# A two-layer vision tower on one core: how the chosen rows of the layer-0 feed-forward are turned

## The chip, the cores and the metric

The kernel runs on one core of one Trainium2 chip, in one launch. The metric is the device time of the whole execution in microseconds (us). Before the change three runs took 1913.69, 1913.17 and 1910.04 us; the median is 1913.17 us.

## The reference, cut to what matters

32 images become 256 tokens of 256 features each. They pass a tokenizer, layer 0 (attention, then a feed-forward part) and layer 1 (attention, then an expert feed-forward part). All data are 32-bit floats. The change touches one product of the layer-0 feed-forward, the one with `w1`:

```
# x: 32 images x 256 tokens x 256 features, after a layer norm
weights = einsum('bsd,do->bso', x, wr) + br          # one weight per token
idx     = top_k(weights, 128)[:, :127]               # 127 tokens of each image
sel     = x[idx]                                     # rows chosen
h       = gelu(sel @ w1 + b1)                        # 256 -> 1024
y       = (h @ w2 + b2) * weights[idx]               # 1024 -> 256
out     = zeros.at[idx].set(y) + x
```

For `sel @ w1` the kernel puts features on partitions (they are summed over) and tokens on the free axis, but the chosen rows lie in memory with tokens on partitions. So they must be turned.

## The kernel before, in words

An image is kept as a tile of 128 partitions (tokens) by 2 by 256. The kernel runs five stages one after the other: A, the tokenizer; B, layer-0 attention with the ranking of tokens; C, the layer-0 feed-forward; D, layer-1 attention; E, the layer-1 feed-forward. The order of the instructions on each engine is that of the program text, in A to D: a hand-written order, with no planner. Each engine and each DMA queue takes its instructions in that order.

**Stage B** goes by pairs of images, in steps `t` of 0 to 17. A step holds work of several pairs: the first products of pair `t`, the attention of pair `t-1`, the output of pair `t-2`, and the ranking of earlier pairs. Pair `t+1` is prepared in the same step. `blocks_b` (L262) turns its tokens with VectorE block transposes: each square of 32 partitions by 32 elements is transposed in place. The result goes to DRAM and comes back with four transfers each way (`turned_b`), so that features lie on partitions. The ranking gives each token its place, and an indirect DMA writes the tokens to a DRAM tensor `ranked` in the order of rank. The first 128 rows of `ranked` are what stage C needs.

**Stage C** goes by quads of four images, eight quads, in steps `t` of 0 to 31. The table `ORDER_C` (L877) is the written order: a row `(step, function, half)` means that the function runs for quad `u` in step `4u + step`, and within a step the rows run in the order of the table. For a quad:

- `first_ranks` (step -8; for quads 0 and 1 in stage B) loads the 128 first rows of four images to a tile `cs` (two buffers) with four transfers on the SP queue.
- `turn_c` (step -1; for quad 0 in the last step of stage B) does eight TensorE transposes of 128 by 128 to two PSUM banks, and copies them to the tile `xsel`, one with ScalarE and one with VectorE.
- `hidden_c` (steps 0 and 1) multiplies by `w1`: 16 products of 128 by 128 with 128 by 512 (the four images' 128 tokens side by side), each followed by a ScalarE gelu.
- `made` (steps 2 and 3, two images each) multiplies by `w2`. VectorE adds the bias into a tile `cy`, and the SP queue writes `cy` to DRAM as `results`.
- `fetch` (steps 4 and 5) gathers `results` back by rank with indirect DMAs of GpSimd, and `update` (steps 5 and 6) adds them to the token tile `h` on VectorE and takes the statistics for the next layer norm.

So in steady state TensorE does, for a quad: transposes, the second `made` of the quad before, two halves of `hidden_c`, the first `made`. There is one `xsel` tile. From step 8 on, a few small products that prepare weights for the later stages (`prepare`) are put between the steps. At the border of B and C the SP queue loads the weights of the later stages, some twenty transfers, and steps 0 and 1 still rank the last images.

Of the kernel before, what the change touches and what calls it, by code (L numbers as in the profile page):

```python
# [33 lines left out]
F32 = mybir.dt.float32  # L34
# [6 lines left out]
P = 128  # L41
B, N, D = 32, 256, 256
NC = N // P
# [37 lines left out]
def vit_tower(tc, a, out):  # L81

    nc = tc.nc
# [7 lines left out]
    ident = cpool.tile([P, P], F32, name="ident")  # L91
# [5 lines left out]
    def bank():  # L97
        return ppool.tile([P, 512], F32, name="bank", tag="bank")
# [16 lines left out]
    def mm(o, lhsT, rhs, first=True, last=True):  # L115
        nc.tensor.matmul(o, lhsT, rhs, start=first, stop=last)  # L116
# [63 lines left out]
    def transposed(xT, xs, copy):  # L180
# [3 lines left out]
        for k in range(2):  # L184
# [4 lines left out]
                    nc.tensor.transpose(p[:, o : o + P], x[:, c, k * P : (k + 1) * P], ident)  # L189
            copy(k, xT[:, k, :], p[:, 0:w])  # L190

    def copy_split(k, o, i):
        if k == 0:
            nc.scalar.copy(o, i)
        else:
            nc.vector.tensor_copy(o, i)
# [6 lines left out]
    px = passing_x.enter_context(tc.tile_pool(name="c_x", bufs=1, reuse_waits="tile"))  # L203
    pdram = passing_x.enter_context(tc.tile_pool(name="c_d", bufs=1, space=bass.MemoryType.DRAM))
# [8 lines left out]
    p0 = region_c0.enter_context(tc.tile_pool(name="c_0", bufs=1, reuse_waits="tile"))  # L213
# [4 lines left out]
    quads = [Quad() for _ in range(B // 4)]  # L218
# [3 lines left out]
        for j in range(4):  # L222
            nc.sync.dma_start(s.x[:, j, :], ranked[b0 + j][0:P, :])

    def turn_c(b0, s, _):
        s.xsel = p0.tile([P, 2, 4 * P], F32, name="xsel")
        for k in range(2):
            p = bank()
            for j in range(4):
                nc.tensor.transpose(p[:, j * P : (j + 1) * P], s.x[:, j, k * P : (k + 1) * P], ident)  # L230
            copy_split(k, s.xsel[:, k, :], p)

    wpool = region.enter_context(tc.tile_pool(name="w_c", bufs=1))
    region_b = ExitStack()
# [26 lines left out]

    def blocks_b(b0, s):  # L262
        s.d = pdram.tile([32, 16 * NC, 4, 32], F32, name="b_turned", bufs=2)
        y = px.tile([P, 8, 2 * NC, 32], F32, name="b_blocks", bufs=1)
        for j, x in enumerate(s.xs):
            nc.vector.transpose(
                y[:, :, j * NC : (j + 1) * NC, :].rearrange("p f c t -> p c f t"),
                x.rearrange("p c (f t) -> p c f t", t=32),
            )
        for i in range(4):  # L270
            nc.sync.dma_start(s.d[:, :, i, :], y[32 * i : 32 * i + 32].rearrange("p f c t -> p (f c) t"))

    def turned_b(b0, s, pool, name):
        s.xT = pool.tile([P, 2, 2 * N], F32, name=name)
        d = s.d.rearrange("q (k f c) i p -> f q k (c i p)", k=2, f=4)
        for f in range(4):
            nc.sync.dma_start(s.xT[32 * f : 32 * f + 32], d[f])
# [12 lines left out]
    with (  # L290
# [7 lines left out]
        for k, n in enumerate(PARTS):  # L298
            f = sum(PARTS[:k])
            x, w = pw.tile([P, n, N], F32, name=f"patch0_{k}"), pw.tile([P, n, D], F32, name=f"tokW{k}")  # L300
# [4 lines left out]
        p = bank()  # L305
# [62 lines left out]
        for b in range(B):  # L368
# [6 lines left out]
            if b == 4:  # L375
                wuv, row_b, wo, row_c, before, w1 = layer_0_weights()
# [45 lines left out]
    with (  # L422
# [96 lines left out]
        for t in range(B // 2 + 2):  # L519
            new, old, older, next_one = pair(t) if t else None, pair(t - 1), pair(t - 2), pair(t + 1)  # L520
            next_one = next_one if t else None
            if t == 1:
                turn_b(*new, p2, "bxT")
            if t >= 4:
                turned = turn_weights(2 * (t - 4))
            if old:
                scores_b(*old)
            if new:
                base_b(*new, p2.tile([P, 2 * N], F32, name="base"))
            if t >= 4:  # L530
                ranks(2 * (t - 4), turned)
                if t in (5, 7):
                    first_ranks(2 * t - 10, quads[t // 2 - 2], 0)
            if new:
                queries_b(*new, p2.tile([P, 2 * N], F32, name="bq"), p2.tile([P, 2 * N], F32, name="bk"))
            if old:
                gates_b(*old)
            if t == 1:
                factors_b(*powers)
            if next_one:  # L540
                norm_b(*next_one)
                blocks_b(*next_one)
            if old and t >= 3:
                norms_c(2 * (t - 3))
            if old:
                values_b(*old)
            if next_one:
                bias_b(*next_one)
            if old and t >= 3:
                residuals_c(2 * (t - 3))  # L550
            if next_one:
                turned_b(*next_one, p2, "bxT")
            if older:
                gated_b(*older)
                if t == B // 2 + 1:
                    turn_c(0, quads[0], 0)
                    norms_c(2 * (t - 3))
                    residuals_c(2 * (t - 3))
                output_b(*older)
# [77 lines left out]
    for i in range(2):  # L637
        s, t = slice(i * HD, (i + 1) * HD), slice((1 - i) * HD, (2 - i) * HD)
# [192 lines left out]
    with region_c:  # L831
        st_d = new_stats("d")

        def hidden_c(b0, s, half):
            if half == 0:
                s.hT = p2.tile([P, 8, 4 * P], F32, name="hT")
            for m in range(4 * half, 4 * half + 4):
                p = bank()
                for k in range(2):
                    mm(p, w1[:, k, m * P : (m + 1) * P], s.xsel[:, k, :], k == 0, k == 1)  # L840
                nc.scalar.activation(s.hT[:, m, :], p, AF.Gelu_apprx_tanh, bias=col("b1", m))

        def made(b0, s, half):
            for j in range(2 * half, 2 * half + 2):
                p = bank()
                for m in range(8):
                    mm(p[:, 0:D], s.hT[:, m, j * P : (j + 1) * P], w2[:, m, :], m == 0, m == 7)
                y = p2.tile([P, D], F32, name="cy", bufs=4)
                nc.vector.tensor_tensor(y, p[:, 0:D], row_c("b2"), ALU.add)
                nc.sync.dma_start(results[b0 + j][:], y)  # L850

        def fetch(b0, s, half):
            s.y = s.y if half else []
            for b in range(b0 + 2 * half, b0 + 2 * half + 2):
                y = px.tile([P, NC, D], F32, name="cx", bufs=8)
                for c in range(NC):
                    k = b * NC + c
                    nc.gpsimd.indirect_dma_start(
                        y[:, c, :], None, results[b][:], bass.IndirectOffsetOnAxis(rank_of[:, k : k + 1], 0)
                    )  # L860
                s.y.append(y)

        def update(b0, s, half):
            for j in range(2 * half, 2 * half + 2):
                b = b0 + j
                st, rs, i = at(st_d, b)
                for c in range(NC):
                    k = b * NC + c
                    nc.vector.scalar_tensor_tensor(  # L869
                        H[b][:, c, :], s.y[j][:, c, :], w_kept[:, k : k + 1], H[b][:, c, :], ALU.mult, ALU.add  # L870
                    )
                    stats(st, i, c, H[b][:, c, :])
            pow_rstd_of(st_d, b0 + 2 * half, 2)

        ORDER_C = ((0, hidden_c, 0), (1, hidden_c, 1), (2, made, 0), (-1, turn_c, 0), (-8, first_ranks, 0),  # L877
                   (3, made, 1), (4, fetch, 0), (5, fetch, 1), (5, update, 0), (6, update, 1))

        def step_c(t):  # L880
            for at_step, do, j in ORDER_C:
                u, r = divmod(t - at_step, 4)
                if r == 0 and 0 <= u < B // 4 and (u > 1 or do is not first_ranks):
                    do(4 * u, quads[u], j)

        END_C = 4 * (B // 4 - 1) + 4
        pairs = [Pair() for _ in range(B // 2)]
        preparing = prepare()
        for t in range(END_C):
            if t == 0:  # L890
                norms_c(B - 2)
                residuals_c(B - 2)
            if t == END_C - 2:
                for u in range(2):
                    norm_d(2 * u, pairs[u], px, "cx", 8)
            step_c(t)
            if t < 2:
                ranks(B - 4 + 2 * t, turn_weights(B - 4 + 2 * t))
            if t >= 8:
                next(preparing, None)  # L900
        passing.close()
# [152 lines left out]
    with (  # L1054
# [452 lines left out]
        p = bank()  # L1507
# [278 lines left out]
def _layout(i):  # L1786


    def blocks(w, p=P):
        k, m = w.shape[0] // p, w.shape[1]  # L1790
        return w.reshape(k, p, m).transpose(1, 0, 2)

    def column(v, p=P):
        return v.reshape(-1, p).T

# [29 lines left out]
    def pairs(w):  # L1825
# [12 lines left out]
        "rows_e": np.concatenate([rows_e[n] for n in ROWS_E]),  # L1838
        "wuv": blocks(i["L0_attn_W_uv"]),
        "wo": blocks(i["L0_attn_W_o"]),  # L1840
        "w1": blocks(i["L0_ffn_w1"]),
        "w2": blocks(i["L0_ffn_w2"]),
        "before": before,
        "wk1": blocks(i["L1_attn_Wk1"]),
# [44 lines left out]
```

## Time and profile before

| What | Value |
|---|---|
| Runs | 1910.04, 1913.17, 1913.69 us, median 1913.17 |
| Profiled execution, its own time | 1911.49 us |
| Its span | 1909.7 us |
| Mean granted TensorE clock | 0.987 |
| TensorE busy | 1864.9 us (98% of the span) |
| VectorE busy | 1313.2 us (69%) |
| ScalarE busy | 805.8 us (42%) |
| GpSimd busy | 757.6 us (40%) |
| Stage C on TensorE | about 681 to 918 us of the span |
| DMA packets | 132226, 109.17 MB |

The profile is of one execution. Its tables name engines as PE (TensorE products), PEld (TensorE weight loads), DVE (VectorE), ACT (ScalarE), POOL (GpSimd) and SPq (the DMA queue of SyncE). L116 is the line of the helper `mm` that issues all products, L230 the line of the transposes in `turn_c`, L189 that of other transposes. A float product appears in the records as two matmuls. Matmuls are pipelined, so the duration of one is longer than the distance to the next; the chain of waits (the work that ended last, followed back from the end) gives the time that they take together. The time of a DMA runs from its issue to its landing.

### The profile page before, as it was taken

The numbers are of one execution on the slowest core, as the hardware profiler recorded it, in microseconds if no ns is written. First come the engines' busy times: TensorE is split into PE (matmuls) and PEld (weight loads), VectorE is DVE, ScalarE is ACT, GpSimd is POOL, SyncE is SP. The second block draws the span as 40 slices with busy tenths as digits, with TensorE's granted clock in tenths as the row PEclk, the third lists the DMA queues.
The fourth block names the chain that finished last, engine by engine and source line by source line (L and its number), as shares of the span: only waits on it lengthen the run. The fifth ranks groups of instructions, "written<-read, shape, count | busy, mean of one in ns | idle before, by whom it ended". The sixth has DMA issues, their size and how long they took to land.

```text
span 1909.7 us, 36912 instructions
## 1 busy us (share of the span) xinstructions
PE 1864.9 (98%) x14740; PEld 1323.7 (69%) x14740; DVE 1313.2 (69%) x3271; ACT 805.8 (42%) x1632; POOL 757.6 (40%) x792
## 2 busy tenths in 40 slices
PE   9999999999999999999989999999999999999993
PEld 8887566666676776766645555567888878787872
DVE  2335478787878563534465555544999999999998
ACT  0001222121212112122334444447787888888772
POOL 1224233333434253424343433324454545555553
PEclk9999999999999999999999999999999999999995
DMA  9550121212121042212000000001222222222211
GB/s 312 151 156 18 35 61 46 71 42 58 47 54 44 34 136 63 82 54 61 15 20 1 1 1 0 1 18 24 58 52 62 58 57 63 52 63 53 64 44 57
DMA packets 132226, 109.17 MB, mean 57 GB/s; under 512 B 67792, under 2 KB 110288, under 8 KB 131664
## 3 DMA queue, kind: packets, MB, share of 16 engines
q1 hardware_dynamic: 125328, 89.17, 17.4%
q0 software_dynamic: 6144, 16.79, 2.8%
q8 instruction: 118, 1.93, 0.4%
q10 hardware_dynamic: 576, 0.79, 0.1%
q14 instruction: 60, 0.49, 0.1%
HBM read 53.75 MB, written 28.31 MB: 43 GB/s over the span
## 4 chain that ended last, share of the span: by engine, by line
PE 94%; DVE 4%; issue 1%; ACT 0%; DMA 0%; SPq 0%; POOL 0%; DVEq 0%; ACTq 0%
PE bank L116 91%; PE bank L792 2%; PE bank L189 1%; PE bank L230 0%; PE bank L500 0%; DVE six L124 0%; DVE fout L1387 0%; DVE fout L1401 0%; DVE eo L1265 0%; DMA b_turned<-b_blocks 0%; DVE ranges L1288 0%; DVE six L987 0%; DVE fout L1390 0%; DMA bxT<-b_turned 0%; DVE h L869 0%
## 5 line engine op out<-in xcount | busy, mean ns | idle before, releaser
L1184 POOL TENSOR_SCALAR_AFFINE_SELECT et<-et 128x512 f32<-128x512 f32 (+1 forms) x192 | 166.2, 878 | 201.6 <-ACT et L1175 199.7
L1175 ACT ACTIVATE et<-bank 128x512 f32<-128x512 f32 x384 | 207.7, 630 | 30.7 <-PE bank L116 30.2
L116 PE MATMUL bank<-ev,et 128*64 128x68 f32 (+1 forms) x6144 | 198.9, 225 | 0.0
L116 PEld LDWEIGHTS bank<-ev,et 128*64 128x64 f32 x6144 | 191.5, 137 | 5.7 <-issue 4.7
L116 PE MATMUL bank<-g,sx 64*128 64x512 f32 (+1 forms) x512 | 177.6, 486 | 0.0
L116 PE MATMUL bank<-g,sw 64*128 64x512 f32 (+1 forms) x512 | 177.2, 486 | 0.0
L116 PE MATMUL bank<-tokW,patch 128*128 128x256 f32 x768 | 167.6, 381 | 0.0
L116 PEld LDWEIGHTS bank<-tokW,patch 128*128 128x128 f32 x768 | 146.6, 191 | 21.4 <-DMA tokW<-in_tokW_dram 0.7
L116 PE MATMUL bank<-bxT,w_wuv 128*128 128x512 f32 x300 | 133.0, 598 | 2.5 <-DMA bxT<-b_turned 2.5
L1204 ACT COPY eo<-bank 128x280 f32<-128x280 f32 x256 | 96.0, 396 | 68.3 <-PE bank L116 61.6
L116 PEld LDWEIGHTS bank<-g,sx 64*128 64x128 f32 x512 | 93.1, 187 | 31.6 <-issue 22.7
L116 PE MATMUL bank<-wvo,dm 128*128 128x512 f32 x256 | 114.3, 599 | 0.0
L116 PE MATMUL bank<-attn,bv 128*128 128x256 f32 x512 | 113.1, 379 | 0.0
L116 PE MATMUL bank<-w_wo,gT 128*128 128x256 f32 x512 | 113.1, 379 | 0.0
L116 PE MATMUL bank<-w_w,hT 128*128 128x256 f32 x512 | 113.1, 379 | 0.0
L116 PE MATMUL bank<-xsel,w_w 128*128 128x512 f32 x256 | 111.4, 593 | 0.0
L116 PEld LDWEIGHTS bank<-attn,bv 128*128 128x128 f32 x512 | 97.2, 190 | 19.6 <-issue 7.2
L124 DVE BATCH_NORM_STATS2 six<-h 128x6 f32<-128x256 f32 x256 | 105.5, 412 | 4.4
L116 PEld LDWEIGHTS bank<-w_w,hT 128*128 128x128 f32 x512 | 96.6, 190 | 15.3 <-issue 2.9
L116 PEld LDWEIGHTS bank<-g,sw 64*128 64x128 f32 x512 | 93.1, 187 | 20.1 <-issue 9.9
L116 PEld LDWEIGHTS bank<-w_wo,gT 128*128 128x128 f32 x512 | 97.2, 190 | 13.2
L116 PE MATMUL bank<-w_wuv,bxT 128*128 128x512 f32 x240 | 105.4, 592 | 0.0
(276 smaller groups left out, 3712.6 us busy)
## 6 DMA issues: line engine op xcount, KB each, us to landing
patch<-in_patches_dram SPq DMA_DIRECT2D x31, 768.0 KB, 4.6
sw<-sx SPq DMA_DIRECT2D x64, 128.0 KB, 2.3
out_dram<-fout SPq DMA_DIRECT2D x32, 256.0 KB, 2.4
both<-fxT SPq DMA_DIRECT2D x62, 128.0 KB, 2.4
both<-hx SPq DMA_DIRECT2D x62, 128.0 KB, 2.3
b_turned<-b_blocks SPq DMA_DIRECT2D x56, 128.0 KB, 3.3
bxT<-b_turned SPq DMA_DIRECT2D x56, 128.0 KB, 3.1
cs<-ranked SPq DMA_DIRECT2D x32, 128.0 KB, 3.5
```

The source lines that it names most:

```text
L116: nc.tensor.matmul(o, lhsT, rhs, start=first, stop=last)
L124: nc.vector.bn_stats(six, x)
L189: nc.tensor.transpose(p[:, o : o + P], x[:, c, k * P : (k + 1) * P], ident)
L792: nc.tensor.transpose(p[:, o : o + P], x[:, c, k * P : (k + 1) * P], ident)
L1175: nc.scalar.activation(t2[:, i, :], p, AF.Exp)
L1184: nc.gpsimd.affine_select(out=own, in_=own, pattern=[[0, 2 * n_e], [1, P]], compare_op=ALU.is_ge, fill=0.0, base=0, channel_multiplier=-1,)
L1204: nc.scalar.copy(im.o[:, g * OC : (g + 1) * OC], p[:, 0:OC])
```

## The change

`turn_c` is replaced by two functions. `blocks_c` transposes a quad's 128 by 1024 tile by squares of 32 on VectorE, in one instruction, into a tile `blocks` (the buffer that stage B uses for the same purpose), and writes it to a DRAM tensor with one transfer on the SP queue, 4 KB from each partition. `moved_c` reads it back into `xsel` with one transfer on the SP queue, in rows of 1 KB, four per partition. After this, feature `128k + 32f + q` lies on partition `4q + f`. The rows of `w1` are put into the same order when the inputs are laid out (`turned`). A quad's tokens now lie in `xsel` in pieces of 32 elements, and the products with `w1` read them as a pattern of 4 by 4 by 32 in place of 512 elements in a row. For quad 0 both functions run in step 15 of stage B (`t == B // 2 - 1`), for the others in steps -3 and -2 of the quad.

```diff
+    def blocks_turned(y, xs, d):
+        y5 = y.rearrange("p (f s t) -> p s f t", f=4, t=32)
+        n = 8 // len(xs)
+        for j, x in enumerate(xs):
+            nc.vector.transpose(
+                y5[:, j * n : (j + 1) * n], x.rearrange("p c (k f t) -> p (c k) f t", k=2, f=4)
+            )
+        nc.sync.dma_start(d.rearrange("i q x -> (i q) x"), y)
+
+    def moved(xT, d):
+        nc.sync.dma_start(xT, d.rearrange("i q (f x) -> (q f) i x", f=4))
+        return xT.rearrange("p i (s k t) -> p k s i t", k=2, t=32)
...
-    def turn_c(b0, s, _):
-        s.xsel = p0.tile([P, 2, 4 * P], F32, name="xsel")
-        for k in range(2):
-            p = bank()
-            for j in range(4):
-                nc.tensor.transpose(p[:, j * P : (j + 1) * P], s.x[:, j, k * P : (k + 1) * P], ident)
-            copy_split(k, s.xsel[:, k, :], p)
+    def blocks_c(b0, s, _):
+        s.d = pdram.tile([4, 32, 4 * N], F32, name="c_turned", bufs=2)
+        blocks_turned(px.tile([P, 4 * N], F32, name="blocks", bufs=1), [s.x], s.d)
+
+    def moved_c(b0, s, _):
+        s.f = moved(p0.tile([P, 4, 2 * P], F32, name="xsel"), s.d)
...
-        y = px.tile([P, 8, 2 * NC, 32], F32, name="b_blocks", bufs=1)
+        y = px.tile([P, 4 * N], F32, name="blocks", bufs=1)
+        y = y.rearrange("p (f c t) -> p f c t", f=8, t=32)
...
+            if t == B // 2 - 1:
+                blocks_c(0, quads[0], 0)
+                moved_c(0, quads[0], 0)
             if older:
                 gated_b(*older)
                 if t == B // 2 + 1:
-                    turn_c(0, quads[0], 0)
                     norms_c(2 * (t - 3))
...
-                    mm(p, w1[:, k, m * P : (m + 1) * P], s.xsel[:, k, :], k == 0, k == 1)
+                    mm(p, w1[:, k, m * P : (m + 1) * P], s.f[:, k], k == 0, k == 1)
...
-        ORDER_C = ((0, hidden_c, 0), (1, hidden_c, 1), (2, made, 0), (-1, turn_c, 0), (-8, first_ranks, 0),
+        ORDER_C = ((0, hidden_c, 0), (1, hidden_c, 1), (2, made, 0), (-3, blocks_c, 0), (-2, moved_c, 0), (-8, first_ranks, 0),
                    (3, made, 1), (4, fetch, 0), (5, fetch, 1), (5, update, 0), (6, update, 1))
...
+    def turned(w):
+        w = blocks(w)
+        return w.reshape(4, 32, *w.shape[1:]).swapaxes(0, 1).reshape(w.shape)
...
-        "w1": blocks(i["L0_ffn_w1"]),
+        "w1": turned(i["L0_ffn_w1"]),
```

## The prediction

> **What bounds the kernel.** I read the page first (engine shares), then the chain of waits over stage C, then the tiles concerned, then the timeline around one turn.
>
> The chain, in its lines of start, length and piece, shows TensorE alone through a quad:
>
> ```profile
> PE 1864.9 (98%) x14740; PEld 1323.7 (69%) x14740; DVE 1313.2 (69%) x3271; ACT 805.8 (42%) x1632; POOL 757.6 (40%) x792
> ...
> 826.17 0.87 PE bank L230 x8
> 827.04 27.55 PE bank L116 x96
> 854.59 0.87 PE bank L230 x8
> 855.46 27.55 PE bank L116 x96
> 883.01 0.87 PE bank L230 x8
> ```
>
> 827.04 + 27.55 = 854.59: the pieces touch. A quad of stage C takes 28.42 us, of which 27.55 are products and 0.87 the eight transposes, and nothing is waited for. So what leaves TensorE here leaves the span, if no wait takes its place. From 827.04 to 854.59 the others have room: VectorE is busy 9.69 us, ScalarE 5.72, GpSimd 10.18 of 27.55, the DMA engines 26%.
>
> The groups of the turn, with min/median/max ns of one:
>
> ```profile
> L230 PE MATMUL bank<-ident,cs x64: 272/273/307, 673.9 to 883.6; 128*128 128x128 f32 x64
> L194 ACT COPY xsel<-bank x9: 585/585/586, 166.7 to 883.5; 128x512 f32<-128x512 f32 x9
> L196 DVE COPY xsel<-bank x9: 669/680/693, 168.4 to 887.6; 128x512 f32<-128x512 f32 x9
> L266 DVE STREAM_TRANSPOSE b_blocks<-cx x28: 661/685/707, 185.1 to 584.6; 128x512 f32<-128x512 f32 x28
> ```
>
> A transpose lasts 273 ns but eight pass in 0.87 us, 109 ns each; the 0.87 is what can be won. The block transpose that the change uses is already there in stage B, at half the size.
>
> The timeline where the new transfer must fit (start, length, engine, idle before in brackets):
>
> ```profile
> 851.17 0.42 DVE L849 TENSOR_TENSOR cy<-bank,rows_c 128x256 f32<-128x256 f32 x1 [9.54 <-PE bank L116]
> 851.62 3.77 SPq L850 DMA_DIRECT2D results<-cy  x2
> ...
> 854.42 1.04 PE L230 MATMUL bank<-ident,cs 128*128 128x128 f32 x8
> 854.62 0.42 DVE L849 TENSOR_TENSOR cy<-bank,rows_c 128x256 f32<-128x256 f32 x1 [3.03 <-PE bank L116]
> ```
>
> The second `results` transfer ends its issue at 851.62 + 3.77 = 855.39, 0.97 us after TensorE finished the first `made` (854.42, where the transposes start). `moved_c` is next on SP.
>
> The transfers that resemble the new ones (size, median us to landing):
>
> ```profile
> patch<-in_patches_dram SPq DMA_DIRECT2D x31, 768.0 KB, 4.6
> b_turned<-b_blocks SPq DMA_DIRECT2D x56, 128.0 KB, 3.3
> bxT<-b_turned SPq DMA_DIRECT2D x56, 128.0 KB, 3.1
> cs<-ranked SPq DMA_DIRECT2D x32, 128.0 KB, 3.5
> results<-cy SPq DMA_DIRECT2D x32, 128.0 KB, 1.7
> ```
>
> **What the Trainium skill says.** "TensorE: Matmul & The Clock Gate", Part 4: PE-mode transpose, says that TensorE is the only path that turns 128 by 128 in one go, that the result is in PSUM and must be copied out, and that one took about 275 ns in a kernel. The trace agrees (273 ns, copies of 585 and 680 ns), but its chain shows 109 ns each when eight follow one another. "VectorE: DVE Perf Modes", The three transpose paths, says that VectorE turns only squares of 32; hence the trip through DRAM. "DMA: Bandwidth & Descriptors", Anatomy of one DMA — SWDGE (gpsimd) path, gives a fixed part of about 2.0 us plus bytes over 436 GB/s. For 512 KB that would be 2.0 + 1.2 = 3.2 us, an estimate. The trace is near it for another kind of queue: 1.7 us at 128 KB where the formula gives 2.3, 4.6 at 768 KB where it gives 3.8. "Advanced Engine Details and Errata", SBUF Cachelines, says that reads keep full speed while following accesses stay in a line of 16 bytes; pieces of 32 floats (128 bytes) do. No run here shows such short pieces on TensorE.
>
> **The change, part by part.**
>
> *Removed from TensorE:* the chain has eight such pieces, seven of 0.87 and one of 0.93 (at 765.90): 7.02 us. For quads 1 to 7 there is no cover, each counts in full. For quad 0 (674.03) the next product needs `gT`, whose four VectorE multiplications run from 673.12 to 675.60. The first is done by about 673.8 and the second by 674.4. Without transposes the product starts at 674.03 and touches the second half about 0.86 us later (four records of 0.215), so I expect no stall; if it waits for both at its start, 0.4 us of the gain is lost. Removed: 6.6 to 7.0.
>
> *Removed from ScalarE and VectorE:* a copy of 585 and one of 680 ns per quad. ScalarE idled 6.7 us before its copy. Worth nothing.
>
> *Added to VectorE:* one block transpose of 1024 elements per quad. Twice the 685 ns row is 1.37 us; if part of the 685 is fixed, less, 1.1 at the lowest. I take 1.3, so VectorE gains 0.6 us per quad. In its order the transpose stands after the second `made`'s two bias additions and before `update`. There VectorE waits 1.20 us for a gather before the update at 835.61, so the transpose fills a hole. Were it not covered, 1.3 us would meet the 9.54 us idle before the next `cy` at 851.17. Queued behind it are that update and GpSimd's small power; nobody on the path. In step 15 of stage B it stands at about 623.9 and pushes a `gT` multiplication from 624.93 by some 0.3 us; VectorE idles 1.03 us before each of the next three. In step 1 of stage C it is tighter: VectorE is busy from 685.19 to 701.50 but for 0.88 us before 696.46. The transpose takes that hole and delays the rest by 0.4, so the bias addition at 701.08 comes later; the next one (703.37) had 1.88 us of idle. Nothing on the path.
>
> *Added to SP:* the write, then the read. The write (512 KB) is issued after the four `cs` loads, which end at about 836.7, and has until about 855.4: 19 us for some 4 us. In step 1 it comes behind the weights (the queue is at 697.3) and lands by about 702, before `moved_c` at about 703.5. At step 15 the queue is empty until 652.9. Only quad 1 is close, by 1.5 us. Two more issues of 0.4 to 0.7 us (patch 0.37, bxT 0.59) delay `results`, whose next waits are for VectorE anyway. While SP waits for the write's landing or for `xsel`, the second `made`'s `results` stand behind it; `fetch` needs them only a step later.
>
> *The read is the critical new step.* It waits for the `results` issue (0.97 us after the first `made`); `xsel` has been free since `hidden_c` ended, 6.9 us before. Then 512 KB in rows of 1 KB. From the rows above: 1.7 us at 128 KB and 4.6 at 768 KB, both in rows of 1 KB, give 1.7 + 384/640 × 2.9 = 3.4 us. The lower bound is 1.7, the size of 128 KB; the upper bound 5.5, as four `cs` loads issued within 1.96 us land (last issue at about 1.5, plus up to 3.9 in that stretch). I take 4.0: landing at 0.97 + 4.0 = 5.0 us. `hidden_c` needs it when the second `made` ends, 27.55 / 4 = 6.89 us. Hidden, with 1.9 us to spare, by the second `made`; at the upper bound still 0.4. Without this cover it would cost its excess seven times (quad 0's is moved some 45 us ahead).
>
> *The products with w1* read pieces of 32. The only other broken moving operand is in layer 1, two pieces of 128 floats:
>
> ```profile
> L116 PE MATMUL bank<-g,sx 64*128 64x256 f32 x256 | 66.0, 377 | 0.0
> L116 PE MATMUL bank<-sx,A 64*128 64x256 f32 x512 | 60.9, 376 | 0.0
> ```
>
> 377 ns against 376 for one in a row: no price. I take none for pieces of 32; the bound above is the second rival.
>
> *Sum:* −7.0 us, 0 for the rest. On the profiled execution: 1911.49 − 7.0 = 1904.5 us (span 1909.7 to 1902.7). The median stands 1.7 us above the profiled time, so 1913.17 − 7.0 = 1906.2; I predict 1906.3, since quad 0 may lose a little.
>
> **Rivals.**
>
> *The read lands late* (10%). For it: it is issued on the last possible occasion, behind a transfer that waits for VectorE, and the `cs` loads of the same bytes reach 4.7 us each. Against it: `fetch` starts only at 860.83, so the DMA engines carry little else at that time. The gain is eaten when it lands 7.9 us after the first `made` (7 × 1.0); a little late, at 7.5, leaves 7.0 − 7 × 0.6 = 2.8: 1910.4 us.
>
> *Short pieces slow the products* (5%), the one on the slow side. The w1 products take 256 records × 0.43 = 110 us of the chain. At 6.4% (430 to 457 ns start to start) the gain is gone. At 12% the balance is +13.2 − 7.0 = +6.2: 1919.4 us. For it: no run shows pieces of 128 bytes. Against it: the two-piece form and the skill's page.
>
> *The gain is partly refilled* (9%): small waits at quad 0, at the crowded VectorE of step 1 and at the start of stage D, 3 us of 7: 1909.2 us. Against it: VectorE and GpSimd in those places wait for TensorE, and so move with it.
>
> **How the numbers follow.** The main case has 76% at 1906.3, own range 1903 to 1908.5 (the runs before spread 3.7 us). About 0.2% (3.8 us) is what a measurement of this kernel tells from no change. Faster: the main case, 75%, and part of the third and first rivals, 5%. Same: most of the first and half of the third, 13%. Slower: the second and a read far too late, 7%. Range 1902.5 to 1911: it takes in the third rival and the mild part of the first; the second and the rest lie above.
>
> **What would show it.** Right: no pieces of L230; quads of 27.55 in the chain from 711 on, touching; a block transpose of 1.1 to 1.4 us on VectorE; the read landing 3.4 to 5.5 us after issue; w1 products still at 592 ns. Wrong: a DMA into `xsel` as releaser of TensorE in the chain, with 0.5 us or more; w1 products above 592 ns; `results` issued visibly later, with VectorE or GpSimd named in the chain of stage C.

## The result, and the profile after

The changed kernel takes 1906.38 us (median of ten runs, 1903.11 to 1906.82), the kernel before 1912.66 (ten runs, 1910.04 to 1914.14). The ratio is 0.9965, with a 95% interval of 0.9955 to 0.9974. The profiled execution took 1904.97 us with a span of 1903.3; the prediction had 1906.3 for the median and 1904.5 for the profiled execution.

The chain of waits through stage C, after a line of the page with the engines' busy times. L514 is the turn of the ranking weights (L500 before), L786 a turn in the preparation of weights, L189 the first turn of layer 1:

```profile
PE 1856.5 (98%) x14676; PEld 1318.8 (69%) x14676; DVE 1311.6 (69%) x3271; ACT 801.1 (42%) x1624; POOL 757.5 (40%) x792
...
670.18 0.44 PE bank L514 x4
670.61 20.77 PE bank L116 x80
691.38 0.44 PE bank L514 x4
691.82 6.87 PE bank L116 x16
698.69 0.44 PE bank L514 x4
699.12 96.58 PE bank L116 x397
795.70 0.44 PE bank L786 x4
796.14 118.82 PE bank L116 x424
914.96 0.45 PE bank L189 x4
```

The pieces touch (670.61 + 20.77 = 691.38, 796.14 + 118.82 = 914.96), and the 0.87 pieces of the turn are gone. TensorE waits for nothing in the stage. From the last pair's first weight turn to the first turn of layer 1 it is 914.96 − 670.18 = 244.78 us. The same two marks in the kernel before:

```profile
666.69 0.44 PE bank L500 x4
...
918.34 0.45 PE bank L189 x4
```

Before it was 918.34 − 666.69 = 251.65 us. The stage gave 6.87 us.

The instructions and transfers that the change touches, as the answers by tile have them (min/median/max ns of one), with the times from issue to landing of the read (L203) in the last line:

```profile
L197 DVE STREAM_TRANSPOSE blocks<-cs x8: 1233/1236/1244, 627.3 to 860.2; 128x1024 f32<-128x1024 f32 x8
L116 PE MATMUL bank<-xsel,w_w x256: 592/592/677, 684.4 to 900.6; 128*128 128x512 f32 x128
...
L203 SPq DMA_DIRECT2D xsel<-c_turned x8: 371/376/1355, 631.2 to 881.5; - x8
...
DMA to landing us min/median/max: 3.7/3.9/4.9
```

And the timeline of one turn, where the read must fit:

```profile
825.45 0.42 DVE L865 TENSOR_TENSOR cy<-bank,rows_c 128x256 f32<-128x256 f32 x1 [3.03 <-PE bank L116]
...
826.33 0.37 SPq L203 DMA_DIRECT2D xsel<-c_turned  x1
...
832.16 4.03 PE L116 MATMUL bank<-xsel,w_w 128*128 128x512 f32 x9
...
832.70 1.23 DVE L197 STREAM_TRANSPOSE blocks<-cs 128x1024 f32<-128x1024 f32 x1
```

The bias addition at 825.45 starts 0.2 us after TensorE ends the first `made`. The read is issued at 826.33, lands 3.9 us later at 830.2, and is needed at 832.16: 1.9 us to spare. The slowest of the seven, issued at 853.87, took 4.9 us and landed at 858.8 for products at 859.70: 0.9 us to spare.

The spans differ by 6.4 us, not by 6.87, since two places outside the stage differ between these two executions. Stage A ends some 3.5 us later in the changed kernel's profile: its first patches land later, and the products behind them start at a lower granted clock (0.84 from 9 to 20 us). A stretch of layer 1 is 3.0 us longer in the profile of before. The second profiles below show that neither belongs to a kernel.

### The profile page after: what moved, and what is told of

Same layout as the page of the kernel before. It is cut to its first block, busy times and chain, and to the rows that moved or that the text cites. A ratio compares the mean times of both kernels' runs of the same rounds, so it can differ in the third digit from the quotient of the medians.

```text
span 1903.3 us, 36813 instructions
## 1 busy us (share of the span) xinstructions
PE 1856.5 (98%) x14676; PEld 1318.8 (69%) x14676; DVE 1311.6 (69%) x3271; ACT 801.1 (42%) x1624; POOL 757.5 (40%) x792
## 4 chain that ended last, share of the span: by engine, by line
PE 94%; DVE 4%; DMA 1%; issue 1%; ACT 0%; SPq 0%; POOL 0%; DVEq 0%; ACTq 0%
PE bank L116 91%; PE bank L808 2%; PE bank L189 1%; DMA patch<-in_patches_dram 0%; PE bank L514 0%; DVE six L124 0%; DVE fout L1403 0%; DVE fout L1417 0%; DVE eo L1281 0%; DMA b_turned<-blocks 0%; DVE ranges L1304 0%; DMA bxT<-b_turned 0%; DVE six L1003 0%; DVE fout L1406 0%; DVE h L885 0%
## 5 line engine op out<-in xcount | busy, mean ns | idle before, releaser
L857 ACT ACTIVATE hT<-bank,cols 128x512 f32<-128x512 f32 x64 | 44.0, 687 | 186.7 <-PE bank L116 186.7
L116 PEld LDWEIGHTS bank<-w_w,hT 128*128 128x128 f32 x512 | 97.1, 190 | 15.4 <-issue 2.9
```

## The experiments

Times are against the changed kernel's 1906.4. Ratios are against the kernel before, run beside each experiment on the same chip; the medians of the kernel before lay within 1 us of 1912.7 there.

**The turns put back as dead work.**

```diff
+    def dead_turns(b0, s, _):
+        for k in range(2):
+            p = bank()
+            for j in range(4):
+                nc.tensor.transpose(p[:, j * P : (j + 1) * P], s.x[:, j, k * P : (k + 1) * P], ident)
...
-        ORDER_C = (..., (2, made, 0), (-3, blocks_c, 0), ...
+        ORDER_C = (..., (2, made, 0), (-1, dead_turns, 0), (-3, blocks_c, 0), ...
```

> The changed kernel, with the eight TensorE transposes of each quad put back where they were, into two PSUM banks that nobody reads; the new transfers stay, the copies stay out. Theory (the gain is TensorE's time of the turns, and the read is hidden): 8 x 0.87 us come back, 1906.4 + 7.0 = 1913.4, no difference from the kernel before, and the pieces of 0.87 stand again in the chain. Rival (part of the gain came from the copies that left ScalarE and VectorE, or from another place): 1908 to 1911, below the kernel before by what the copies were worth.

Measured: 1913.37 us, ratio 1.0001 (0.9992 to 1.0009). For quad 0 the same function runs in the last step of stage B. The chain of this kernel:

```profile
667.96 0.44 PE bank L520 x4
...
827.44 0.87 PE bank L250 x8
828.31 27.55 PE bank L116 x96
855.86 0.87 PE bank L250 x8
...
919.61 0.45 PE bank L189 x4
```

The pieces of 0.87 are back, the stage takes 919.61 − 667.96 = 251.65 us as before, and nothing of the gain is left. So all of it was TensorE's time; the copies that left ScalarE and VectorE, and the transfers that came, are worth nothing here.

**The read issued without cover.**

```diff
-        ORDER_C = (..., (-2, moved_c, 0), (-8, first_ranks, 0), (3, made, 1), (4, fetch, 0), ...
+        ORDER_C = (..., (-8, first_ranks, 0), (3, made, 1), (-1, moved_c, 0), (4, fetch, 0), ...
```

> The changed kernel, with the read issued after the second made of the quad before instead of after its first, so that no product lies between it and the products with w1. Theory (issue 1.0 us after TensorE, landing 3.9 us later, and the second made's 6.9 us are the whole cover): TensorE waits 4.9 us in each of seven quads, less where the small weight products of three or four quads lie between: about 30 us, 1936 us, with the DMA into xsel as releaser of TensorE. A clock that falls in such waits could add some us. Rival (the read is covered by something else as well, as by products queued ahead): under 10 us.

Measured: 1967.78 us, 61.4 us slower than the changed kernel, twice what was expected. Two of the seven waits in the timeline:

```profile
714.86 16.54 PE L116 MATMUL bank<-xsel,w_w 128*128 128x512 f32 x32 [4.97 <-DMA xsel<-c_turned]
...
869.92 15.83 PE L116 MATMUL bank<-xsel,w_w 128*128 128x512 f32 x32 [7.80 <-DMA xsel<-c_turned]
```

The first quad waits 4.97 us, as worked out. The later ones wait 5.5 to 7.8, because the read now takes 4.5 to 6.9 us in the chain instead of 3.9. Gathers and the loads of `cs` are issued around it there (from 861.44 and at 863.50, the read at 863.03); that they slow it was not tried. All seven waits sum to 44.6 us. Small weight products stand before only two of them and covered 1.2 and 1.9 us there. The second surprise is in the length of each line (its second number): the products after a wait take 15.4 to 16.5 us for 32 records where the changed kernel's take 13.9 to 14.0. The seven together are some 13.6 us longer, and the mean granted clock over these records is 0.84 to 0.91. 44.6 + 13.6 = 58.2 of the 59.8 us by which the stage is longer (971.68 − 667.12 = 304.56). The cover is real, and a wait of TensorE costs some 30% more than its length here (13.6 beside 44.6).

**The read issued early.**

```diff
-        ORDER_C = (..., (2, made, 0), (-3, blocks_c, 0), (-2, moved_c, 0), ...
+        ORDER_C = (..., (-2, moved_c, 0), (2, made, 0), (-3, blocks_c, 0), ...
```

> The changed kernel, with the read issued before the first made's results in SP's order, 7 us earlier. Theory (hidden already): no change, 1906.4 within 2 us. Rival (the late read costs some tenths of a us per quad, hidden in the chain as products): 2 to 5 us faster, 1902 to 1904.

Measured: 1905.47 us, ratio 0.9962 (0.9948 to 0.9975) beside 0.9965 for the change. The stage takes 911.96 − 667.16 = 244.80 us. No difference: the late place of the read costs nothing.

**The read done twice.**

```diff
+        xT = p0.tile([P, 4, 2 * P], F32, name="xsel")
+        if b0:
+            moved(xT, s.d)
+        s.f = moved(xT, s.d)
```

> The changed kernel, with the read of quads 1 to 7 done twice, the second into the same tile after the first has landed. Theory (cover of 6.9 us, 1.0 used before the issue): the second lands at 1.0 + 2 x 3.9 + about 0.1 = 8.9 us after the first made, 2.0 us late in each of the quads without small weight products in between: 7 x 2.0 = 14 us at most, 10 us if three quads are covered; 1916 to 1921 us. Rival (the margin is really near zero, so that the whole second read is late): 7 x 3.9 = 27 us, 1933.

Measured: 1922.04 us, 15.6 us slower than the changed kernel and just above the range that the theory gave. Two of five waits in the timeline:

```profile
714.39 13.97 PE L116 MATMUL bank<-xsel,w_w 128*128 128x512 f32 x32 [2.13 <-DMA xsel<-c_turned]
744.16 14.00 PE L116 MATMUL bank<-xsel,w_w 128*128 128x512 f32 x32 [1.99 <-DMA xsel<-c_turned]
```

Five quads wait 2.13, 1.99, 2.17, 3.22 and 2.44 us, 11.9 in all, and two wait for nothing, as small weight products lie between. One stretch of products after a wait is 1.7 us longer (15.70). That makes 13.6 of the 15.6; the other 2 us are within the spread of the runs. Three of the waits are near the 2.0 that the sum of cover and landing gives; in the other two the reads took longer in the chain (4.97 and 4.18 us, 4.03 and 4.29). So the spare 1.9 us of the changed kernel is confirmed from the other side.

**The pieces of the moving operand.** Three kernels read the same 512 columns in another order, in pieces of one, two and four floats. The line of 16 bytes in the expectations is the one that the prediction cites from the Trainium skill.

```diff
-        return xT.rearrange("p i (s k t) -> p k s i t", k=2, t=32)
+        return xT.rearrange("p i (s k t) -> p k t s i", k=2, t=32)                 # pieces of one
+        return xT.rearrange("p i (s k a b) -> p k a (i s) b", s=4, k=2, b=2)       # of two; of four with b=4
```

> The changed kernel, with the products with w1 reading their moving operand as 32 by 4 by 4 instead of 4 by 4 by 32, so that each float comes from another place, 1 KB from the last. The 512 columns are the same in another order, so the rows of the four images of a quad are mixed in the feed-forward part: only the time is read. Theory (broken reads cost nothing at the pace of float products here, 430 ns for 512 columns): 592 ns per record and 1906 us, no change. Rival (a read pays per line of 16 bytes, and pieces of 32 floats only hid it): each of 256 records gets longer; at twice the time 256 x 0.43 = 110 us, 2016 us.

Measured: 2015.58 us, 109 us slower than the changed kernel.

> The changed kernel, with the moving operand of the products with w1 read in pieces of two floats, each 256 bytes from the last. As with pieces of one, the 512 columns come in another order, so the four images' rows are mixed in the feed-forward part; only the time is read. Theory (a second access to the same line of 16 bytes makes up for the first): 592 ns per record and 1906 us. Rival (each change of line costs, in proportion): half of the price of pieces of one, 592 + 215 = about 810 ns per record and 1961 us.

Measured: 1903.76 us, ratio 0.9954 (0.9940 to 0.9967).

> As before with pieces of four floats, a full line of 16 bytes; the images' rows are mixed in the same way. Theory: 592 ns per record and 1906 us. Rival (in proportion): 592 + 108 = about 700 ns per record and 1934 us.

Measured: 1905.34 us, ratio 0.9960 (0.9946 to 0.9973). The products with `w1` in the kernel with pieces of one:

```profile
L116 PE MATMUL bank<-xsel,w_w x256: 1019/1037/1086, 682.6 to 1008.9; 128*128 128x512 f32 x128
...
696.98 13.77 PE bank L116 x16
```

The last line is of its chain, where the changed kernel has 6.87 us for the same sixteen. With pieces of two:

```profile
L116 PE MATMUL bank<-xsel,w_w x256: 592/593/680, 682.6 to 899.7; 128*128 128x512 f32 x128
```

A record of pieces of one takes 1037 ns instead of 592. From start to start it is 13.77 / 16 = 0.86 us instead of 0.43, and 256 × 0.43 = 110 us is what the stage lost (1023.74 − 668.42 = 355.32 us instead of 244.78). Pieces of two cost next to nothing: their stage takes 914.07 − 668.41 = 245.66 us, 0.9 us more than the changed kernel's, or 3 ns per record. Pieces of four cost nothing (912.99 − 668.20 = 244.79). So the rival of the prediction that ended on the slow side exists as a mechanism, but only at single floats. (The pieces of one lie 1 KB apart and those of two 256 bytes; whether the distance plays a part was not tried.)

**The two kernels again, for second profiles.**

> The kernel before, unchanged, for a second profile. The two profiles at hand differ in two places the change doesn't touch: the first patches land 3.5 us later in the changed kernel's profile, and a stretch of layer-1 attention (1000 to 1010) runs at a granted clock of 0.67 in the profile of before alone. Theory (both are of the single execution): this profile shows other values in at least one of the two. Rival (both belong to the kernels): the clock falls again at about 1000, and the start is as fast as before.

> The changed kernel, unchanged, for a second profile. Theory: stage C from the first weight turn of the last pair to the first turn of layer 1 takes 244.8 us again (251.7 before), whatever the start and the clock do. Rival: the start of the kernel is 3.5 us later again and the clock does not fall, so that these belong to the change.

Measured: 1913.35 us (before) and 1906.33 (after). In the stretch of layer 1 the first profile of before has in its chain

```profile
1000.45 20.83 PE bank L116 x62
```

and the second

```profile
1003.77 17.84 PE bank L116 x62
```

The changed kernel's two profiles have 17.84 and 20.87 there. So each kernel shows both values: after the same wait for `dxT` the granted clock over these records is 0.85 in some executions and 1.00 in others, which makes 3.0 us. The second profile of before also waits for its first patches (6.81 us in the chain, products going on from 8.69), as both of the changed kernel do. The stage between the markers is 919.94 − 668.28 = 251.66 us and 913.42 − 668.63 = 244.79. The difference of 6.87 repeats to 0.01 us; the late start and the fall of the clock are of the single execution, as both kernels show them.

**The same turn in layer-1 attention.** Pairs 2 to 15 of stage D get block transposes, one write and one read as well.

```diff
...
+        def blocks_d(b0, s):
+            s.d = pdram.tile([4, 32, 4 * N], F32, name="d_turned", bufs=2)
+            blocks_turned(px.tile([P, 4 * N], F32, name="blocks", bufs=1), s.xs, s.d)
+
+        def moved_d(b0, s):
+            if b0 > 2:
+                s.f = moved(p2.tile([P, 4 * N], F32, name="dxT").rearrange("p (i x) -> p i x", i=4), s.d)
+            else:
+                turn(b0, s)
...
-                    mm(p, (wk1, wq1)[i][:, k, m * P : (m + 1) * P], s.xT[:, k, :], k == 0, k == 1)
+                    mm(p, ((wk1, wq1) if b0 <= 2 else (wk1t, wq1t))[i][:, k, m * P : (m + 1) * P], s.f[:, k], k == 0, k == 1)
...
-                do(1, turn)
+                do(1, moved_d)
...
-                do(0, norm_d, p8, "dx", 4)
+                do(-1, norm_d, p8, "dx", 6)
+                do(-1, blocks_d)
...
```

> The changed kernel, with the same turn in layer-1 attention for pairs 2 to 15: normalised tokens one step earlier (six buffers for four), block transposes, one write, one read, a second set of the first-layer weights in the new order of features; pairs 0 and 1 keep TensorE's transposes. Theory (same mechanism, 0.87 us per pair in a chain of TensorE alone): 14 x 0.87 = 12 us faster than the changed kernel, 1894 us. Rival (VectorE, which is busy 57% there and sets the chain at the start of the stage, or the two steps of cover for two transfers that need about 10 us, give some of it back): 1900 to 1906, with VectorE or a DMA in the chain of that stage.

Measured: 1885.47 us, ratio 0.9859 (0.9843 to 0.9876); 20.9 us faster than the changed kernel where 12 were expected. Its chain in layer 1 has

```profile
989.27 238.40 PE bank L116 x952
```

238 us of products follow each other without a turn or a wait. At the start of the stage TensorE waits twice. The first two lines are the changed kernel's, the others this kernel's:

```profile
973.16 2.84 PE L116 MATMUL bank<-dxT,w_wk 128*128 128x512 f32 x6 [2.43 <-DVE dxT L210]
996.99 2.84 PE L116 MATMUL bank<-dxT,w_wk 128*128 128x512 f32 x6 [2.55 <-DVE dxT L210]
...
968.64 3.67 PE L116 MATMUL bank<-dxT,w_wq1t 128*128 128x512 f32 x8 [0.28 <-DVE h L1026]
989.27 3.67 PE L116 MATMUL bank<-dxT,w_wq1t 128*128 128x512 f32 x8 [0.26 <-DVE h L1026]
```
Stage D takes 1238.29 − 911.76 = 326.5 us, from its first turn to the first products of the next stage. In the changed kernel it is 343.3 (1258.22 − 914.96), and 344.7 in the kernel with the early read: 16.7 to 18.2 us less. In TensorE's own time 12.2 us of that are the fourteen turns. Another 4.4 are the two waits: the copy into `dxT`, which stood behind other VectorE work, is gone from these pairs. 12.2 + 4.4 = 16.6 of the 16.7; beside the kernel with the early read it is 1.5 more, as that one had a lower clock (0.92) after the first wait. The rest of the 20.9 us lies outside the stage. Between the two profiles 3.2 us of it stand before stage C (670.18 beside 666.97), which this change does not touch: the changed kernel's first profile has two stretches of slower products there (160.79 beside 159.11 us for 736 records, 61.89 beside 60.49 for 208). This version beats both kernels.

## Why the prediction was right, point by point

- *Removed from TensorE, 6.6 to 7.0 us, taken as 7.0:* 6.87 by the chain. Quad 0 gave 0.79: from the weight turn's end to the next one's start it was 688.68 − 667.12 = 21.56 before and is 20.77. So the wait for both halves of `gT`, which might have cost 0.4, did not come; only 0.08 was lost. The other seven gave 6.87 − 0.79 = 6.08, 0.87 each. The piece of 0.93 was counted 0.06 too high.
- *Copies worth nothing:* shown by the dead turns, which bring the whole time back with the copies still left out.
- *Block transpose, 1.3 us:* 1.236. It is less than twice the 685 ns row, as a fixed part allowed. At 832.70 it lies behind the second bias addition and before the update. The sum of waits of `update` for its gathers grew from 9.4 to 15.1 us, on an engine that waits anyway; none of it is in the chain of the stage.
- *The write, some 4 us:* 2.6 to 4.4. The closest one, quad 1's, was issued at 700.84 and had until 706.95.
- *The read, 4.0 us, issued 0.97 after the first made:* 3.9, issued 1.1 after. The working from two sizes gave 3.4, and the 4.0 was then taken between this and the upper bound of 5.5 without a working of its own; that it fell so near is in part luck. The spare was put at 1.9 and is 1.9 in the median, 0.9 at worst.
- *Pieces of 32 cost nothing:* 592 ns, unchanged.
- *The rivals:* the read did not land late, the pieces did not slow the products, and nothing was refilled. What the first would have cost was mis-sized: the prediction took a late read at its excess, seven times over. The experiment without cover shows that the read is slower in another place and that the clock falls after a wait, so that an expected 4.9 us of lateness became 8.8 per quad.

The total agrees to 0.1 us with the median, closer than the argument earns: the runs spread by 3.7 us, and over ten runs the kernel before has a median of 1912.66, not the 1913.17 that the prediction started from. The forecast drop of about 6.9 us is 6.3 by the medians and 6.87 by the chain. That the profiled execution came within 0.5 us is luck as well, as its late start (3.5 us) and the slow stretch in the profile of before (3.0) nearly cancel.

## What to carry to other kernels

Where TensorE is the whole chain of a stage, a turn moved to VectorE's block transposes and a trip through DRAM gave back just the turn's place in the chain (0.87 us for eight), not the sum of its durations; what has to be shown is the cover, from the issue's last releaser to the first use. The order of features is free if the weights can be laid out in it, and a broken moving operand cost here nothing in pieces of four floats or more and under 1% in pieces of two. Look for the same turn elsewhere in the kernel: in layer 1 it also removed a copy that stood in a queue behind other work.

## What the hardware showed unexpectedly

- A moving operand of float products in single floats, 1 KB apart, takes 860 ns from start to start for 512 columns instead of 430, double; pieces of two, 256 bytes apart, are within 1% of full speed. The Trainium skill, "Advanced Engine Details and Errata", SBUF Cachelines, asks for at least two hits on a line of 16 bytes; the measured step between one and two agrees with it, as far as the distance plays no part.
- After each of seven waits of TensorE of 5 to 8 us the granted clock was 0.84 to 0.91 of full speed over the next 32 records, about 1.9 us lost per wait. After a wait of some 2.5 us it fell in some executions of the same kernel and not in others (20.83 and 17.84 us for the same 62 records).
- In the last experiment the same normalising instruction of VectorE (L835, 128 by 256) takes 921 ns on average in its new place instead of 410. The trace shows two kinds: of each four, two pass in 0.76 us together and the next two in 2.77 us, and these lie beside two long additions of GpSimd (1052.95 to 1055.57). The block transposes behind them lie beside such additions too and keep their 683 ns. That the additions are the cause was not tried.
